# Toeplitz passes of a four-layer network kernel moved: the first beside the second half of the projections, the second beside image 0's front, with weights rearranged and its loads on ScalarE's queue

## The chip, the core and the metric

The kernel runs on one core of one Trainium2 chip. The metric is the device time of one execution in microseconds (us). A NeuronCore has TensorE (PE in the profile, with PEld for its weight loads), VectorE (DVE), ScalarE (ACT), GpSimd (POOL) and SyncE (SP); SP, ACT and POOL also issue DMA transfers, each from its own queue, in program order.

## What is computed

The input is eight images of 56 x 56 pixels with 192 channels, in float32. Four residual layers follow one another, each behind a group norm: a Toeplitz gated layer, window attention, a depthwise 3 x 3 convolution, and a selective scan in four directions. The change concerns the first layer and small tables of the second to fourth. The first layer, cut to what matters:

```
def _gn(v, G=32, eps=1e-5): ...          # group norm without scale and shift
p = silu(x @ p_w.T + p_b)                # x is the normalised image
q = silu(x @ q_w.T + q_b)
v = silu(x @ v_w.T + v_b)                # 576 channels each
qv = q * v
o1 = toeplitz(qv along the rows, a1)     # per channel, a 56 x 56 Toeplitz matrix
o2 = toeplitz(qv along the columns, a2)
x  = x + (p * (o1 + o2)) @ o_w.T + o_b
...
x  = x + window_attention(_gn(x))        # 7 x 7 windows, shifted by 3, bias table, mask
x  = x + depthwise_conv3x3(_gn(x))
x  = x + selective_scan_block(_gn(x))    # projection, conv, 4 scans of 3136 steps, 16 states
```

## The kernel before

All data between the stages lies in HBM. The kernel first makes the Toeplitz generators (`ext`, lines 157 to 203), and then works in two halves of the images: `now` is 0 to 3, `later` 4 to 7.

`products` (line 206) makes q * v. For each image it loads x (L217), takes the group norm (`group_stats`, L130 to L150), normalises into `xn` with a row of ones for the bias (L220, L153), and then, for each of 25 token tiles, multiplies 3 x 384 output columns in two steps of the 192 channels (L234, L235), applies Silu on ACT (L236), multiplies on DVE (L237), and stores four tiles at a time to `qv` (L240). Its `yield 4.3` after each token tile hands a cost in us to whoever drives it.

`toeplitz` (line 246) goes over two axes and six blocks of 96 channels. Two rows (or columns) of an image share the 112 partitions. It loads a block of all four images into `tzx` (8 DMAs, L268), and for every 24 channels a block-diagonal tile of generators into `tm` (2 DMAs, L277). Four channels make a unit: four matmuls of 112 x 112 weights with 112 moving columns (L281), then one copy back into `tzx` (L287, in turn on DVE and ACT when it runs alone, on DVE otherwise), and `yield 1.0`. There are 288 units for four images. Both matmul operands are strided: the weights are `t[:, :, c2 + c]` of a tile [112, 112, 24], the moving columns `x[:, :, c]` of a tile [112, 112, 96]. Results go out by 8 DMAs on POOL's queue (L295) per block.

The driver runs `products(now)` and `toeplitz(now)` to their ends, one after the other. Then come the constants of the rest (L302 to L349), and small tables: the attention bias from 98 DMAs on ACT's queue (L360), four mask additions (L365), convolution taps (L379), and borders of the padded images (L392), all in a buffer `slab` that the front uses next.

`front(b)` is image b's way up to the scan, a generator of small steps: `gate` (first layer's end), `attention`, `conv2`, `inner` (projection and convolution of the scan block) and `steps` (its time steps). For b = 0 a driver at the end of the listing runs it with the products and then the Toeplitz of 4 to 7 (`others`): each front step's engine costs, from a table of prices, times 0.55 is what `others` may spend. After that the scan begins, in an order written out by hand (`manual_schedule`), with the fronts of images 1 to 7 fitted between its instructions by the same prices; the change doesn't touch that part. Outside it, a scheduler orders each engine's instructions, so that program order is only near to the source's order.

Image 0's front is compiled through a helper that records prices, so most of its instructions stand under line 83 in the profile.

Of the kernel before, what the change touches and what calls it, by code (L numbers as in the profile page):

```python
# [15 lines left out]
F32 = mybir.dt.float32  # L16
AF = mybir.ActivationFunctionType
# [71 lines left out]
def model(ctx: ExitStack, tc: tile.TileContext, a: dict, out: bass.AP):  # L89
# [40 lines left out]
    def group_stats(x, sp, ps, mean_out, rstd_out):  # L130

        st = sp.tile([CP, 2, NCH, 6], F32, name="gn_st")
        mv = sp.tile([CP, 2, 2], F32, name="gn_mv")
        for k in range(2):
            for j in range(NCH):
                nc.vector.bn_stats(out=st[:, k, j, :], in_=x[:, k, j * CH : (j + 1) * CH])
            nc.vector.bn_aggr(out=mv[:, k, :], in_=st[:, k].rearrange("p j s -> p (j s)"))
        pm = ps.tile([128, 512], F32, name="ps_gn", tag="ps")
        nc.tensor.matmul(pm[:CP, 0:2], gmat, mv[:, :, 0], start=True, stop=True)
        nc.vector.tensor_copy(mean_out, pm[:CP, 0:2])  # L140

        dm = sp.tile([CP, 2], F32, name="gn_dm")
        nc.vector.tensor_sub(dm, mv[:, :, 0], mean_out)
        nc.vector.tensor_mul(dm, dm, dm)
        nc.vector.tensor_add(dm, dm, mv[:, :, 1])
        pv = ps.tile([128, 512], F32, name="ps_gn", tag="ps")
        nc.tensor.matmul(pv[:CP, 0:2], gmat, dm, start=True, stop=True)
        sd = sp.tile([CP, 2], F32, name="gn_sd")
        nc.scalar.activation(sd, pv[:CP, 0:2], AF.Sqrt, bias=eps5[:CP])
        nc.vector.reciprocal(rstd_out, sd)  # L150
# [54 lines left out]
    def products(images, beside):  # L205
        with (
# [8 lines left out]
            for b in images:  # L215
                x = sp.tile([CP, 2, L], F32, name="x0", bufs=1 if beside else 2)
                nc.sync.dma_start(out=x, in_=blocks(a["x"][b]))  # L217
                group_stats(x, sp, ps, stats0[:, b, :, 0], stats0[:, b, :, 1])
                xn = sp.tile([CP + 1, 2, L], F32, name="xn0")
                nc.gpsimd.memset(xn[CP : CP + 1, 1, :], 1.0)  # L220

                for k in range(2):
                    normalize(xn[:CP, k, ::-1], x[:, k], stats0[:, b, k, 0:1], stats0[:, b, k, 1:2])
                for t0 in range(0, L, 512):
# [3 lines left out]
                    for t in range(n_t):  # L228
                        tok = slice(t0 + t * p_t, t0 + (t + 1) * p_t)
                        sl = sp.tile([128, 2 * D1], F32, name="sl", bufs=3)  # L230
# [15 lines left out]
    def toeplitz(images, beside):  # L246
        G = len(images) * (H // 2)
        with (
            tc.tile_pool(name="tz", bufs=2) as sp,
            tc.tile_pool(name="tz_t", bufs=1) as tp,  # L250
            tc.tile_pool(name="tz_ps", bufs=4 if beside else 8, space=PSUM) as ps,
        ):

            tm = [tp.tile([TT, TT, TC], F32, name=f"tm{i}") for i in range(3)]
            for t in tm:
                nc.gpsimd.memset(t, 0.0)
            n_t = 0
            for ax in range(2):
                along_h = "(h u w) c -> u h w c"
                along_w = "(u h w) c -> u w h c"  # L260
                stored = "(w u h) c -> u w h c"
                size = dict(h=H, u=2) if ax == 0 else dict(w=W, u=2)
                for c0 in range(D1 // CP):
                    x = sp.tile([TT, G, CP], F32, name="tzx", bufs=2 if beside else 3)
                    for n, b in enumerate(images):
                        v = qv_d[b][c0].rearrange(along_w if ax else along_h, **size)
                        for u in range(2):
                            nc.sync.dma_start(out=x[u * W : (u + 1) * W, n * 28 : (n + 1) * 28, :], in_=v[u])  # L268
                    for c1 in range(0, CP, TC):
                        t = tm[n_t % 3]  # L270
                        n_t += 1
                        e = ext[1 - ax][(c0 * CP + c1) // TC]

                        src = bass.AP(e.tensor, e.offset, [[TC, W], [1, W * TC]])
                        for u in range(2):
                            dst = t[u * W : (u + 1) * W, u * W : (u + 1) * W, :].rearrange("p i c -> p (i c)")
                            nc.sync.dma_start(out=dst, in_=src)  # L277
                        for c2 in range(0, TC, 4):
                            po = ps.tile([TT, 4, G], F32, name="ps_tz")
                            for c in range(4):  # L280
                                nc.tensor.matmul(  # L281
                                    po[:, c, :], t[:, :, c2 + c], x[:, :, c1 + c2 + c], start=True, stop=True
                                )
                            cs = slice(c1 + c2, c1 + c2 + 4)
                            copy = nc.vector.tensor_copy if (c2 // 4) % 2 or beside else nc.scalar.copy

                            copy(  # L287
                                x[:, :, cs].rearrange("p (b g) c -> p b g c", g=28)[:, :, ::-1, :],
                                po.rearrange("p c (b g) -> p b g c", g=28),
                            )  # L290
                            yield 1.0
                    for n, b in enumerate(images):
                        v = o_d[ax][b][c0].rearrange(stored if ax else along_h, **size)
                        for u in range(2):
                            nc.gpsimd.dma_start(out=v[1 - u], in_=x[u * W : (u + 1) * W, n * 28 : (n + 1) * 28, :])  # L295
# [3 lines left out]
    for stage in (products, toeplitz):  # L299
        for _ in stage(now, False):  # L300
            pass


    with (
# [45 lines left out]


        bias, bmask, masks = carve(slab, PT_, (NH, WS, 2, WS), (4, 6, PT_), (4, PT_))
        nc.sync.dma_start(out=masks, in_=a["masks"])

        nc.gpsimd.memset(bias, 0.0)
        for i in range(WS):
            for u in range(2):
                for j in range(WS):
                    at = (i * 2 + u) * WS + j
                    nc.scalar.dma_start(  # L360
                        out=bias[at : at + 1, :, :, u, :],
                        in_=a["table"][:, WS - 1 - i : 2 * WS - 1 - i, WS - 1 - j : 2 * WS - 1 - j].unsqueeze(0),
                    )
        for m in range(4):
            nc.vector.tensor_add(  # L365
                bmask[:, m],
                bias.rearrange("p a i u j -> p a (i u j)"),
                masks[:, m : m + 1, :].to_broadcast([PT_, 6, PT_]),
            )
        nc.sync.dma_start(out=bmask_d, in_=bmask)  # L370
        ident3, cw2, cw3, dg2, dg3, edge = carve(
            slab, 128, (32,), (C // 32, 3), (DI // 32, 3), (C // 32, 3, 32), (DI // 32, 3, 32), (2, WP)
        )
        nc.sync.dma_start(out=ident3[:CP], in_=a["ident3"])
        for cw, dg, dg_d in ((cw2, dg2, dg2_d), (cw3, dg3, dg3_d)):
            n = cw.shape[1]
            nc.sync.dma_start(out=cw[:CP], in_=a["cw2" if n == C // 32 else "cw3"])
            for dx in range(3):
                nc.vector.tensor_mul(  # L379
                    dg[:CP, :, dx, :],  # L380
                    ident3[:CP].unsqueeze(1).to_broadcast([CP, n, 32]),
                    cw[:CP, :, dx : dx + 1].to_broadcast([CP, n, 32]),
                )
            nc.sync.dma_start(out=dg_d, in_=dg[:CP])

        nc.gpsimd.memset(edge, 0.0)
        for pads in (pad2_d, pad3_d):
            for pad in pads:
                n = CP if pads is pad2_d else 128
                for c in range(0, pad.shape[0], n):  # L390
                    v = pad[c : c + n].rearrange("p (h w) -> p h w", w=WP)
                    nc.scalar.dma_start(out=v[:, 0 : H + 2 : H + 1, :], in_=edge[:n])  # L392
# [807 lines left out]
        with tc.tile_pool(name="ps0", bufs=4 if later else 8, space=PSUM) as ps:  # L1200
            log = costs.setdefault("front", [])
            first, others, spent = front(0), (us for stage in (products, toeplitz) for us in stage(later, True)), 0.0
            while log_of(first, log) is not None:
                spent += 0.55 * sum(cost for _, cost in log[-1])
                while later and spent > 0.0:
                    us = next(others, None)
                    if us is None:
                        break
                    spent -= us
            for _ in others if later else ():  # L1210
                pass
# [213 lines left out]
```

## Time and profile before

| what | value |
|---|---|
| median of 3 runs | 21627.49 us (21618.97 to 21637.12) |
| the profiled execution | 21638.53 us, its span 21636.7 us |
| mean granted TensorE clock | 0.862 of full |
| PE busy | 17516.4 us (81%) |
| POOL busy | 15086.4 us (70%) |
| DVE busy | 15781.2 us (73%) |
| ACT busy | 12150.2 us (56%) |
| first matmul of the scan stage | about 3450 us after the start |

The profile is of one execution. Busy time is the time in which an engine has at least one instruction of the program at work; a busy engine may still be waiting for data inside an instruction. "Idle before" a group of instructions, and what ended it, tells what an engine waited for. PEclk is the TensorE clock granted, as a share of full. A matmul in float32 stands as two records.

### The profile page before, as it was taken

To read this page: it belongs to the slowest core of one execution; us is meant where nothing else is said; L and a number is where in the kernel's file an instruction comes from. 1 tells how busy PE (TensorE), PEld (TensorE's weight loads), DVE (VectorE), ACT (ScalarE), POOL (GpSimd) and SP (SyncE) were. 2 spreads that over 40 slices of the span, in tenths; PEclk is the share of its full clock that TensorE was granted. 3 is DMA by queue.
4 is the path that set the end of the run, shared out by engine and by line. 5 is a ranking of instruction groups with operands and counts; after the bars stand their busy time and mean duration, and the time that the engine had idled before them with its cause. 6 is when DMAs were issued, how large, how long until landed. Compare 5 with 4: busy or idle time off the path is not lost. (4 is left out here: it accounts for less than half of the span.)

```text
span 21636.7 us, 198667 instructions
## 1 busy us (share of the span) xinstructions
PE 17516.4 (81%) x59404; PEld 9109.9 (42%) x59404; DVE 15781.2 (73%) x12469; ACT 12150.2 (56%) x28249; POOL 15086.4 (70%) x9176
## 2 busy tenths in 40 slices
PE   7878678887887788878887888788878888777777
PEld 4845465433443344334433444344433443333333
DVE  2122116986798779967896789778977887788998
ACT  3126113666666666656665667476656665755555
POOL 0000005886788778867886788678877887799998
PEclk9587658988998899888998899889988998888888
DMA  3931676456544655475446654665466546644443
GB/s 87 244 98 39 193 211 176 131 161 211 173 138 145 217 171 148 134 220 174 138 139 206 192 143 126 206 196 146 133 201 195 145 132 189 202 134 132 138 137 115
DMA packets 2566491, 3470.12 MB, mean 160 GB/s; under 512 B 936270, under 2 KB 2518704, under 8 KB 2534578
## 3 DMA queue, kind: packets, MB, share of 16 engines
q1 hardware_dynamic: 2542724, 3340.61, 52.0%
q0 software_dynamic: 15520, 116.14, 1.5%
q8 instruction: 473, 7.75, 0.2%
q14 instruction: 606, 4.96, 0.1%
q10 hardware_dynamic: 7168, 0.65, 0.0%
HBM read 2822.68 MB, written 634.11 MB: 160 GB/s over the span
## 5 line engine op out<-in xcount | busy, mean ns | idle before, releaser
L1106 PE MATMUL ps_y<-hc,ident_sb 128*128 128x448 f32 x21504 | 10046.0, 605 | 966.8 <-POOL hc L1091 957.4
L1059 POOL TENSOR_TENSOR ring<-du,bm 128x896 f32<-128x896 f32 x5376 | 9459.7, 1774 | 1870.1 <-ACT ring L1066 1736.1
L1076 ACT ACTIVATE ps_a<-delta,A_logs_sb 128x449 f32<-128x449 f32 x10752 | 6859.5, 638 | 314.3 <-DVE ring L1085 57.7
L1106 PEld LDWEIGHTS ps_y<-hc,ident_sb 128*128 128x128 f32 x21504 | 4331.0, 211 | 5336.0 <-issue 3600.1
L1085 DVE TENSOR_TENSOR_SCAN ps_a<-ps_a,ring 128x898 f32<-128x898 f32 x2688 | 5429.7, 2020 | 954.6 <-ACT ring L1066 485.6
L1085 DVE TENSOR_TENSOR_SCAN ring<-ps_a,ring 128x898 f32<-128x898 f32 x2688 | 5422.1, 2017 | 488.2 <-ACT state L1098 180.6
L1091 POOL TENSOR_TENSOR hc<-ring,cm 128x896 f32<-128x896 f32 x2688 | 4767.2, 1774 | 898.9 <-DVE ring L1085 497.3
L1091 DVE TENSOR_TENSOR hc<-ps_a,cm 128x896 f32<-128x896 f32 x2688 | 2934.0, 1092 | 950.7 <-PE ps_y L1106 725.3
L1098 ACT COPY state<-ps_a 128x2 f32<-128x2 f32 x2687 | 426.2, 159 | 2932.4 <-DVE hc L1091 2926.2
L287 DVE COPY tzx<-ps_tz 112x448 f32<-112x448 f32 x432 | 269.8, 624 | 1456.4 <-PE ps_tz L281 1261.2
L281 PE MATMUL ps_tz<-tzx,tm 112*112 112x112 f32 x4608 | 1031.4, 405 | 348.6 <-DMA tm<-ext 280.2
L295 POOL DMA_DIRECT2D o<-tzx x192 | 97.3, 513 | 1593.9 <-DVE tzx L287 1510.2
L281 PEld LDWEIGHTS ps_tz<-tzx,tm 112*112 112x112 f32 x4608 | 1021.8, 319 | 389.5 <-issue 385.5
L1098 ACT COPY state<-ring 128x2 f32<-128x2 f32 x2688 | 504.2, 188 | 663.7 <-DVE ring L1085 644.3
L666 PE MATMUL ps_f<-ident_sb,slab 98*98 98x98 f32 x1344 | 333.4, 328 | 628.5 <-ACT slab L659 626.1
L1042 POOL TENSOR_TENSOR du<-delta,xcd 128x448 f32<-128x448 f32 x672 | 659.4, 981 | 19.5 <-DMA slab<-in_w_p_dram 19.4
L83 PE MATMUL ps_f<-slab 96*32 96x448 f32 (+7 forms) x2432 | 604.2, 569 | 71.2 <-DMA slab<-pad 51.5
L1066 ACT COPY ring<-state 128x6 f32<-128x6 f32 x1536 | 292.8, 191 | 629.0 <-POOL ring L1059 627.7
L666 PEld LDWEIGHTS ps_f<-ident_sb,slab 98*98 98x98 f32 x1344 | 205.2, 159 | 1032.7 <-ACT slab L659 813.1
L234 PE MATMUL ps_qv<-wqv,xn 96*128 96x384 f32 (+1 forms) x1200 | 530.1, 525 | 131.1 <-DVE xn L153 67.5
L503 PE MATMUL ps_f<-ident_sb,slab 112*96 112x112 f32 x4704 | 529.1, 267 | 101.0 <-DVE slab L511 53.5
L503 PEld LDWEIGHTS ps_f<-ident_sb,slab 112*96 112x96 f32 x4704 | 506.6, 169 | 240.3 <-issue 105.5
(221 smaller groups left out, 16312.2 us busy)
## 6 DMA issues: line engine op xcount, KB each, us to landing
bm<-bc SPq DMA_DIRECT2D x1792, 448.0 KB
cm<-bc SPq DMA_DIRECT2D x1792, 448.0 KB
xcd<-xc SPq DMA_DIRECT2D x840, 224.0 KB
dl<-slab SPq DMA_DIRECT2D x224, 672.0 KB
delta<-dl SPq DMA_DIRECT2D x224, 672.0 KB
slab<-pad SPq DMA_DIRECT2D x504, 232.0 KB
tzx<-qv SPq DMA_DIRECT2D x192, 588.0 KB
o<-tzx POOLq DMA_DIRECT2D x192, 588.0 KB, 13.8
```

The source lines that it names most:

```text
L83: return f(*args, **kw)
L234: nc.tensor.matmul(pq[:p_t], xn[:CP, 0, tok], wqv[:CP, 0, col], start=True, stop=False)
L281: nc.tensor.matmul(po[:, c, :], t[:, :, c2 + c], x[:, :, c1 + c2 + c], start=True, stop=True)
L503: nc.tensor.matmul(p[:CP, t * TT : (t + 1) * TT], ot[:, n % 2, i, t, c % 2 * CP : c % 2 * CP + CP], ident[:TT, :TT], start=i == 0, stop=i ...
L666: nc.tensor.transpose(p[:PT_, e * PT_ : (e + 1) * PT_], S[:, 3 * g + e, :], ident[:PT_, :PT_])
L1042: nc.gpsimd.tensor_mul(du[:, 0, :], deltas[i][:, d, 1 : CH + 1], xcs.pop((i, d)))
L1059: nc.gpsimd.tensor_mul(hs[:, :, tokens(i)[0]], dus[i, d].to_broadcast([128, NG, CH]), bms[i, k])
L1076: nc.scalar.activation(dA[:, n, :], deltas[i][:, d, at : at + CH + 1], AF.Exp, scale=negA[:, slot, d, c : c + 1])
L1085: nc.vector.tensor_tensor_scan(h, dA, hs, 0.0, ALU.mult, ALU.add)
L1091: (nc.gpsimd if on_pool(d, k) else nc.vector).tensor_mul(hc, h[:, :, tokens(i)[0]], cms[i, k])
L1098: nc.scalar.copy(states[i][:, d, NG * k : NG * k + NG], h[:, :, tokens(i)[2]])
L1106: nc.tensor.matmul(yps[i, d][:, :CH], ident, hcs[g][:, n, :], start=k + n == 0, stop=k + n == NP + NG - 2)
```

## The change

It has six parts.

1. `toeplitz` fetches each generator tile into one of two row tiles `tr`, and POOL copies it into `tm`, [112, 24, 112], so that a channel's weights are contiguous; the fetch is one chunk ahead. A block of `tzx` is loaded when the block before is half done. It has two `tzx` buffers and four PSUM buffers always, and all copies back are on DVE. The queue of its loads is an argument.
2. `products(later)` runs with `toeplitz(now)` fed in between, at 0.47 of its price; each image is normed and normalised in two halves with single buffers.
3. `toeplitz(later)` runs beside `front(0)`, at 0.29 of the front's price, with its loads on ACT's queue.
4. Bias table, masks, taps and borders are made during `products(now)`, in a pool of their own, with the 98 table loads and the borders on POOL's queue.
5. `group_stats` takes one or two blocks of channels.
6. A driver `beside` does the feeding for both.

```
-    def toeplitz(images, beside):
+    def toeplitz(images, queue):
...
+            rows = [tp.tile([TT, TT, TC], F32, name=f"tr{i}") for i in range(2)]
...
+            def fetch(n):
...
+                for u in range(2):
+                    dst = tr[u * W : (u + 1) * W, u * W : (u + 1) * W, :].rearrange("p i c -> p (i c)")
+                    queue.dma_start(out=dst, in_=src)
+                tms[n] = sp.tile([TT, TC, TT], F32, name="tm")
+                nc.gpsimd.tensor_copy(tms[n].rearrange("p c i -> p i c"), tr)
...
+            load(0)
+            fetch(0)
...
+                for c1 in range(0, CP, TC):
+                    fetch(n_t + 1)
+                    t = tms.pop(n_t)
+                    n_t += 1
+                    if c1 == 2 * TC:
+                        load(m + 1)
...
-                                    po[:, c, :], t[:, :, c2 + c], x[:, :, c1 + c2 + c], start=True, stop=True
+                                po[:, c, :], t[:, c2 + c, :], x[:, :, c1 + c2 + c], start=True, stop=True
...
-                            copy = nc.vector.tensor_copy if (c2 // 4) % 2 or beside else nc.scalar.copy
+                        nc.vector.tensor_copy(
...
-    for stage in (products, toeplitz):
-        for _ in stage(now, False):
+        for n, _ in enumerate(products(now, False)):
+            if n == 8:
...
+                            nc.gpsimd.dma_start(
+                                out=bias[at : at + 1, :, :, u, :],
...
+    def beside(work, other, share):
+        due = 0.0
+        for us in work:
+            due += share * us
+            while due > 0.0:
+                due -= next(other, due)
+        for _ in other:
+            pass
+
+    first = toeplitz(now, nc.sync)
+    next(first)
+    beside(products(later, True), first, 0.47)
...
-                    nc.scalar.dma_start(
-                        out=bias[at : at + 1, :, :, u, :],
...
-            first, others, spent = front(0), (us for stage in (products, toeplitz) for us in stage(later, True)), 0.0
-            while log_of(first, log) is not None:
-                spent += 0.55 * sum(cost for _, cost in log[-1])
...
+            priced = (sum(cost for _, cost in log[-1]) for _ in iter(lambda: log_of(first, log), None))
+            beside(priced, toeplitz(later, nc.scalar), 0.29)
```

In `products`, for the images 4 to 7:

```
+                K = 1 if beside else 2
+                for k0 in range(0, 2, K):
+                    x = sp.tile([CP, K, L], F32, name="x0", bufs=1 if beside else 2)
+                    nc.sync.dma_start(out=x, in_=blocks(a["x"][b])[:, k0 : k0 + K])
+                    group_stats(x, sp, ps, stats0[:, b, k0 : k0 + K, 0], stats0[:, b, k0 : k0 + K, 1])
...
+                    if beside:
+                        yield 12.0
```

## The prediction

> **What bounds the kernel now.** I read the page's slices first. The last 34 of 40 look alike: the scan of the selective-scan layer, with POOL, DVE and PE each at 70 to 90%. The change doesn't touch an instruction of it. The first six slices, some 3450 us, look different: POOL and DVE are nearly idle and the granted clock (PEclk) falls to half. I cut them at the borders of the stages in a table of windows. The columns are the stretch, its length, the busy time of PE, PEld, DVE, ACT and POOL, PEclk, the DMA share and GB/s.
>
> ```profile
> core 0: us, PE busy (x) PEld busy (x) DVE busy (x) ACT busy (x) POOL busy (x), PEclk, DMA share, GB/s
> ...
> 86.00:504.00 418.00, 402.63 (x1212) 229.90 (x1212) 112.67 (x168) 153.26 (x307) 5.41 (x2) 0.97 0.32 81
> 504.00:534.00 30.00, 0.00 (x0) 0.00 (x0) 0.00 (x0) 0.00 (x0) 6.90 (x3) 0.50 0.84 195
> 534.00:1112.00 578.00, 510.76 (x2304) 507.90 (x2304) 89.92 (x144) 76.65 (x144) 44.65 (x88) 0.50 0.87 232
> 1112.00:1246.00 134.00, 0.93 (x4) 0.79 (x4) 13.80 (x30) 4.47 (x5) 10.00 (x11) 0.50 0.30 81
> 1246.00:1570.00 324.00, 321.43 (x1395) 194.08 (x1396) 90.28 (x147) 93.14 (x150) 2.91 (x2) 0.97 0.44 106
> 1570.00:2203.00 633.00, 569.90 (x2178) 320.91 (x2179) 159.03 (x327) 387.80 (x1066) 2.71 (x1) 0.80 0.22 54
> 2203.00:2365.00 162.00, 96.52 (x485) 34.41 (x479) 20.78 (x37) 27.57 (x37) 6.90 (x3) 0.74 0.74 197
> 2365.00:2740.00 375.00, 262.78 (x1123) 190.98 (x1124) 52.11 (x86) 56.83 (x71) 12.14 (x24) 0.63 0.66 201
> 2740.00:3175.00 435.00, 324.45 (x1131) 244.28 (x1129) 68.93 (x111) 91.59 (x113) 20.29 (x40) 0.58 0.71 207
> 3175.00:3390.00 215.00, 170.24 (x768) 169.29 (x768) 59.95 (x96) 0.00 (x0) 15.95 (x32) 0.50 0.76 184
> 3390.00:3450.00 60.00, 4.50 (x25) 4.30 (x26) 8.65 (x8) 8.26 (x16) 17.47 (x15) 0.50 0.92 285
> ```
>
> The stages are: products of images 0-3 (PE-bound, DMA a third busy); their Toeplitz products alone (534 to 1112, DMA at 87%); a hole of 134 us; image 0's gate (to 1570) and attention (to 2203) with products of 4-7 mixed in; its convolution, inner projection and steps (to 3175) with Toeplitz of 4-7; that Toeplitz's rest alone; the scan's start. PE's 510 us of the lone Toeplitz are one matmul after another.
>
> The next view is the source view of four lines (min/median/max in ns): the Toeplitz matmul L281, the projection L234, and L503, which has the same 112 moving columns but reads them and its weights contiguously.
>
> ```profile
> L281 PEld LDWEIGHTS ps_tz<-tzx,tm x4608: 293/320/323, 534.2 to 3384.7; 112*112 112x112 f32 x192
> ...
> L234 PE MATMUL ps_qv<-wqv,xn x1200: 482/486/1009, 86.1 to 2201.2; 96*128 96x384 f32 x165, 96*64 96x384 f32 x7
> ...
> L503 PEld LDWEIGHTS ps_f<-ident_sb,slab x672: 159/163/283, 3473.6 to 3844.3; 112*96 112x96 f32 x168
> ...
> L360 ACTq DMA_DIRECT2D slab<-in_table_dram x98: 714/718/1354, 1141.6 to 1238.9; - x98
> ```
>
> An fp32 matmul is two records: 1152 matmuls per four images stand as 2304. L281's weight load never takes under 293 ns, at either clock. Lone Toeplitz records start 220 ns apart at half clock, and also at full clock (57 records in 13.15 us, 2412 to 2436, PEclk 1.00). L503's start 96 ns apart. So L281 is held by its operands' reads, not by the clock. L360 is the hole: 98 tiny loads issued one by one on ScalarE's queue, 97 us, with the Sqrt of image 4's norm behind them. In attention (activation groups by form):
>
> ```profile
> L236 ACT ACT_TABLE_LOAD x38 | 48.8, 1283 | 0.7
> L83 ACT ACT_TABLE_LOAD x36 | 46.2, 1283 | 3.1 <-DVE mxs L83 2.6
> ```
>
> Silu of the products and Exp of attention swap tables, 95 us of ACT.
>
> **What the Trainium skill says.** "SBUF — State Buffer", Door 1, says SBUF lines are 16 bytes and each access that goes to a new line pays; four fp32 is the free stride. L281's weights step 96 bytes and its moving columns 384. The trace agrees for the weights (293 ns against 163). "TensorE: Matmul & The Clock Gate", Part 1, says the clock is half or full, set by how busy PE was in windows of about 3.4 us; the trace agrees (0.50 in the lone Toeplitz, 1.00 where it alternates with dense matmuls at 2412). "DMA: Bandwidth & Descriptors", Issuing engines are not separate DMA queues, says another queue saves the issue time alone; the transfers share the engines. No run here shows it for these loads. "GPSIMD Engine Reference", section 7, prices a widely strided read at 2.9 cycles an element; no copy of this kind is in the trace.
>
> **The change, part by part.** All times are against the profiled execution: 21638.5 us, span 21636.7. The median of the runs, 21627.5, is 11 below.
>
> *Weights rearranged.* POOL copies each 2688-element chunk so that a channel's weights are contiguous. Bounds: 2.3 us (the memset of that size) to 6.5 us (2688 x 2.9 cycles at 1.2 GHz, an estimate from the GPSIMD page). At 5 us, 48 copies a pass are 240 us on a POOL that is under 10% busy here; each is issued a chunk ahead of use, and a chunk is 48 records, at least 9 us of PE, which hides it. Were the cover gone, the cost would be those 240 us. What PE gains: a contiguous load of 112 would take about 175 ns (163 at 96 columns) and no longer binds. The moving columns stay strided. Two records that stood alone at full clock ended 263 ns after their load; L503's end 180 after. That puts the moving side near 180 to 190 ns a record. I take 187; the ends are 96 (as L503) and 220 (no gain). A unit of four matmuls is 8 x 187 = 1.5 us; 288 units are 432 us instead of 507.
>
> *Products 4-7 beside Toeplitz 0-3* (instead of the lone Toeplitz). The changed program's PE order shows 246 units among the 600 product matmuls and 42 after them. Products: 1200 records x 323 ns (their spacing at full clock) = 388. Units among them: 246 x 1.5 = 368. The 42 alone at today's lone pace, since transfers bind there: 578/288 = 2.0 us, 84. Four image starts with single buffers and twice the small norm steps: 20. Sum 860 in place of 578. Transfers are no bound: 0.87 x 578 + 0.32 x 418 = 637 us of DMA. New waits: SP's Toeplitz loads wait for their buffer's stores with the stores of the products behind them, which have two buffers of four token tiles, 28 us of PE, as slack; POOL's stores wait for DVE with the next copy behind them, a chunk ahead. DVE has 288 copies of 625 ns plus products, about 300. ScalarE's copies all go to DVE. Start: 35 for 30 (one POOL copy).
>
> *The hole.* The 98 table loads go to POOL's queue during products 0-3, 98 x 0.51 us (the POOL issue of L295) = 50 us on an idle engine; 97 if uncovered. The masks, taps and borders move there too, on DVE, SP and POOL, all free. What is late next is the landing of the last Toeplitz stores (20 us today), the constants and gate's first loads: 45 in place of 134.
>
> *Gate and attention beside Toeplitz 4-7.* In the PE order the last unit stands before attention's end, so all 288 lie here. PE's own front work, by spacing of records, is 187 + 234 = 421; with 432 of Toeplitz 853. Idle PE today is 957 - 891 = 66; I keep it. ScalarE loses 147 us of Silu and the 95 of tables and gets the loads: 96 of x at 1.4 us and 96 of weights at 0.39 (SP's medians) = 172 us; 324 with back-pressure, SP's sum today. In front of them wait image 0's Exp and Identity; behind those, PE. They are spread singly, so I charge 40. Sum 960 in place of 957. SP's queue loses them, so front loads no longer stand behind them.
>
> *Convolution, inner, steps alone*: 972 today. Off go 350 us of L281's PE time there and 60 of 2290 to 2365, when PE waits for the first Toeplitz load. 560. Bounds: 912, if Toeplitz only filled idle slots; 450, since an undisturbed step took 9 us (2788 to 2797) and they average 31.
>
> *Ends.* The lone rest, 215, goes. The scan's start falls from 60 to 30, as the buffers it waits for are long free.
>
> Sum: 504 + 35 + 860 + 45 + 960 + 560 + 30 = 2994, against 3450: 456 less. 21638.5 - 456 = 21182; less 11: about **21170**.
>
> **Rivals.**
> *The stride stays the bound* (220 ns): no trace row shows strided columns over contiguous weights; two records are thin evidence. 152 us back: 21320.
> *Toeplitz only filled holes*: PE idles 28% from 2203 to 3175 today, on DMA round trips. Then that part takes 912 and the time is 21520. Against it: step 9 us against 31.
> *Reads stop binding at all*, 110 ns: 4608 x 77 ns, of which DMA lets through about two thirds: 240 less, 20930.
> *Slower: the clock.* A Toeplitz record fills about half of its 187 ns at full clock. If the mix counts as too idle, all of it runs at half clock. For it: 0.58 to 0.63 from 2365 on. Against: 1.00 at 2412, where two units alternate with dense matmuls, and 0.97 in the gate. Price: products 1200 x (640 - 323) = 380 us (640 is their spacing at half clock), front matmuls about 300. At all of it 21850; it decides from two thirds (456/680).
>
> **From cases to numbers.** Main case 60%, own range 20990 to 21300; stride 15%; holes 10%; no read bound 7%; clock 8%. The range leaves out the clock case and the main case's tails, 18% in all: from the no-read-bound case to the holes case, 20920 to 21530. 0.2% (43 us) is about what a measurement of this kernel can tell from no change. Faster 0.91, same 0.02, slower 0.07.
>
> **What would show it.** Spacing of Toeplitz records near 187 ns; PEclk above 0.9 in the first mix; no hole after it; no ACT table loads in attention beyond a few; steps near 13 us each; the same 18190 us from the scan's start. If the first mix takes over 1000 us, or the part after attention over 800, my sum is wrong there.

## The result, and the profile after

The changed kernel takes 21494.8 us in the median (21475.5 to 21516.5), the kernel before 21628.6 beside it: a ratio of 0.9937, 95% interval 0.9924 to 0.995. That is 134 us less, where 458 were forecast. The profiled execution took 21516.5 us, its span 21514.7.

The windows of the changed kernel from the first mix on, cut at its own stage borders (columns as before):

```profile
core 0: us, PE busy (x) PEld busy (x) DVE busy (x) ACT busy (x) POOL busy (x), PEclk, DMA share, GB/s
...
516.00:1388.00 872.00, 785.52 (x3205) 608.06 (x3205) 353.47 (x458) 158.57 (x316) 248.77 (x125) 0.93 0.76 184
1388.00:1493.00 105.00, 63.45 (x330) 62.84 (x329) 27.98 (x42) 0.00 (x0) 34.38 (x16) 0.79 0.58 136
1493.00:1541.00 48.00, 0.84 (x5) 0.48 (x3) 1.74 (x7) 1.65 (x2) 13.30 (x10) 0.54 0.76 205
1541.00:1905.00 364.00, 346.79 (x1779) 265.20 (x1780) 105.14 (x170) 52.06 (x65) 79.09 (x38) 0.95 0.70 166
1905.00:2700.00 795.00, 541.91 (x2875) 436.82 (x2873) 199.49 (x395) 195.32 (x761) 188.37 (x106) 0.75 0.52 134
2700.00:3050.00 350.00, 194.74 (x957) 76.57 (x956) 29.18 (x60) 87.05 (x115) 0.00 (x0) 0.75 0.66 188
3050.00:3272.00 222.00, 127.71 (x252) 50.62 (x252) 0.00 (x0) 97.46 (x122) 9.84 (x7) 0.58 0.58 192
```

Set against the sum of the prediction, in us of the profiled executions:

| stage | forecast | measured | off by |
|---|---|---|---|
| to the end of products 0-3 | 504 | 474 | -30 |
| start of the first mix | 35 | 42 | +7 |
| products 4-7 beside Toeplitz 0-3, with its lone tail | 860 | 872 + 105 = 977 | +117 |
| transition | 45 | 48 | +3 |
| gate and attention beside Toeplitz 4-7 | 960 | 364 + 795 = 1159 | +199 |
| convolution, inner, steps alone, scan start | 560 + 30 | 350 + 222 + 15 = 587 | -3 |
| scan stage | 18190 | 18228 | +38 |

The misses sum to 331, which is the difference of 21516.5 to the forecast 21182 within 4 us. Two of them, both in the mixes, make up the error. Attention is the larger: there PE is busy for 542 of 795 us.

The operations themselves came out as they were costed (source view; min/median/max in ns):

```profile
L312 PEld LDWEIGHTS ps_tz<-tzx,tm x4608: 172/193/312, 515.6 to 2660.4; 112*112 112x112 f32 x192
...
L279 POOL COPY tm<-tr x96: 4693/4790/6546, 510.8 to 2632.4; 112x2688 f32<-112x2688 f32 x96
```

L312 is the Toeplitz matmul (L281 before), L279 POOL's copy of the weights; the records of L312 start 192 ns apart at full and at half clock. The copy takes 4.8 us where 5 were taken, and the 98 table loads (L345), 0.65 us each in the median, leave POOL's queue between 38 and 107 us.

What ScalarE waited for, from the first to the last softmax of the changed kernel (1905 to 2687 us), and PE in the same stretch (columns: us in total, times, longest):

```profile
ACT slab L83 <- PE ps_f L83: 294.7, 104, 15.8
ACT slab L83 <- DVE mxs L83: 152.3, 58, 17.9
ACT slab L83 <- issue: 83.9, 17, 14.9
ACT slab L83 <- DMA slab<-x: 41.2, 7, 18.7
...
PE ps_f L83 <- ACT slab L83: 183.1, 31, 23.4
PE ps_tz L312 <- POOL tm L279: 58.9, 9, 16.5
```

PE's idle time there is 248 us, and two waits are nearly all of it: 183 for ScalarE and 59 for weights that POOL hasn't copied. ScalarE in turn waits 152 us for DVE's part of the softmax, spends 84 us between instructions without waiting for data ("issue") and loses 41 on late loads of image 0's strips. In the trace, 83 of the 84 us lie under its own issues of loads. This is the source view of the input blocks' loads on its queue, from 1905 us on:

```profile
L296 ACTq DMA_DIRECT2D tzx<-qv x64: 312/327/15406, 1905.9 to 2587.2; - x64
```

The 64 issues of input blocks in attention sum to 127 us (one held the queue for 15.4), the 64 of weight rows to 31. One turn of the loop, from the timeline of the changed kernel:

```profile
2029.58 0.31 ACTq L277 DMA_DIRECT2D tr<-ext  x1
...
2030.39 0.31 ACTq L277 DMA_DIRECT2D tr<-ext  x1
...
2037.55 9.37 POOL L279 COPY tm<-tr 112x2688 f32<-112x2688 f32 x2 [20.47 <-DMA tr<-ext]
...
2042.31 18.77 PE L312 MATMUL ps_tz<-tzx,tm 112*112 112x112 f32 x96 [6.53 <-POOL tm L279]
...
2061.66 0.18 DVE L83 RECIPROCAL mxs<-mxs 98x6 f32<-98x6 f32 x1
2061.87 1.71 ACT L83 ACTIVATE slab<-slab,mxs 98x98 f32<-98x98 f32 x6 [17.85 <-DVE mxs L83]
```

A row's load leaves ScalarE only behind attention's copies; POOL waits for it; PE stands 6.5 us before the first unit and then runs 96 records; the softmax's reciprocal stands on DVE behind the units' copies back; and ScalarE, which has the next row's load to issue, waits 17.9 us for the reciprocal. So late weights and the units' copies back reach the softmax through DVE too.

### The profile page after: what moved, and what is told of

The parts are those of the page before. It is cut to its first block, busy times and chain, and to the rows that moved or that the text cites. A ratio compares the mean times of both kernels' runs of the same rounds, so it can differ in the third digit from the quotient of the medians.

```text
span 21514.7 us, 198772 instructions
## 1 busy us (share of the span) xinstructions
PE 17346.1 (81%) x59420; PEld 8955.4 (42%) x59420; DVE 15957.1 (74%) x12633; ACT 12003.9 (56%) x28043; POOL 15598.6 (73%) x9378
## 5 line engine op out<-in xcount | busy, mean ns | idle before, releaser
L279 POOL COPY tm<-tr 112x2688 f32<-112x2688 f32 x96 | 458.6, 4799 | 1116.8 <-DMA tr<-ext 642.8
L312 PE MATMUL ps_tz<-tzx,tm 112*112 112x112 f32 x4608 | 925.8, 370 | 183.6 <-POOL tm L279 178.0
L312 PEld LDWEIGHTS ps_tz<-tzx,tm 112*112 112x112 f32 x4608 | 868.8, 202 | 233.3 <-POOL tm L279 185.5
L316 DVE COPY tzx<-ps_tz 112x448 f32<-112x448 f32 x576 | 356.9, 622 | 741.5 <-PE ps_tz L312 715.4
L241 ACT ACTIVATE sl<-ps_qv 128x384 f32<-128x384 f32 x600 | 293.5, 491 | 753.7 <-PE ps_qv L240 609.2
L242 DVE TENSOR_TENSOR qv<-sl 128x576 f32<-128x576 f32 (+1 forms) x200 | 207.7, 1041 | 573.8 <-ACT sl L241 554.5
```

What stands on the lines that cost most here:

```text
L279: nc.gpsimd.tensor_copy(tms[n].rearrange("p c i -> p i c"), tr)
L312: nc.tensor.matmul(po[:, c, :], t[:, c2 + c, :], x[:, :, c1 + c2 + c], start=True, stop=True)
```

## The experiments

Ratios are to the kernel before, timed beside each, with their 95% intervals; the changed kernel's is 0.9937 (0.9924 to 0.995). Us worked out from a difference of two ratios are uncertain by some 40. Stage times are of one trace each. "Softmax" is the stretch from the first to the last of image 0's 32 softmaxes, with the Toeplitz units that ran in it; 782 us and 203 units in the changed kernel.

### Which part brings what

**e1_sp.** All loads of Toeplitz 4-7 on SyncE's queue.

```
-            beside(priced, toeplitz(later, nc.scalar), 0.29)
+            beside(priced, toeplitz(later, nc.sync), 0.29)
```

> Changed kernel with one word changed: the loads of Toeplitz 4-7 (input blocks and weight rows) are issued on SyncE's queue instead of ScalarE's. Theory Q (in the changed kernel each weight row's load waits in ScalarE's order behind image 0's activations, these wait for PE and DVE, and both stand behind the Toeplitz units that wait for the row): the rows land before they are needed, gate and attention beside Toeplitz 4-7 go from 1160 us to 960-1020, the time from 21495 to about 21320 (21280 to 21370). Theory C (the order in which the scheduler placed the units, in clumps of 25 to 96 matmuls inside attention's chain, costs the time whatever queue loads them): the stage stays within 40 us of 1160, time 21455 to 21535. Theory S (SyncE's strip loads and stores now stand behind row loads that wait for a free row buffer): the stage gets longer, time over 21550.

Measured: 0.9856 (0.9843 to 0.987), 21352 us: one word is worth 0.81%, some 175 us by the ratios; in the two traces the scan starts 145 us earlier (3142 for 3287). Softmax took 447 us with 104 units; the other 96 units went behind attention, and that part grew from 600 to 800. Waits of the same stretch (1894 to 2341):

```profile
ACT slab L83 <- PE ps_f L83: 171.9, 132, 7.3
ACT slab L83 <- DVE mxs L83: 84.1, 61, 3.3
ACT slab L83 <- DMA slab<-x: 0.8, 2, 0.6
PE ps_f L83 <- ACT slab L83: 74.7, 27, 5.2
PE ps_tz L312 <- POOL tm L279: 1.0, 1, 1.0
```

ScalarE's issue time is gone, its waits for DVE are 68 us shorter, and PE idles 76 us in place of 248. But the built order (the one that the scheduler makes) changed with the queue, so queue and placement aren't told apart yet.

**e2_serial.** Toeplitz 4-7 to its end before image 0's parts.

```
-            beside(priced, toeplitz(later, nc.scalar), 0.29)
+            for _ in toeplitz(later, nc.sync):
+                pass
+            for _ in priced:
+                pass
```

> Changed kernel with Toeplitz of images 4-7 run to its end before image 0's parts begin, loads on SyncE's queue, so that the trace has each alone. Tells what mixing is worth. Lone Toeplitz: 2.45 us a unit as in the 42 units after the products (1387 to 1490 us) would be 700 us; 1.54 us a unit (192 ns a record) would be 443. Front alone: PE's own work in gate and attention was counted as 421 us; with attention's round trips I expect 600 to 650. If mixing hides what it can (theories Q and C wrong), the two alone sum to 1350 or more against 1160 and the time is about 21690. If the mix is bad, they sum to 1100-1200 and the time is 21435 to 21540.

Measured: 0.9973 (0.9964 to 0.9982), 21608 us. From the start of the second Toeplitz to the scan it took 1860 us, against 1746 in the changed kernel and 1618 in e1_sp: so the change's mix hides 114 us, and e1_sp's 242. The 21608 us lie between the two cases of the expectation. It is the only trace with attention alone. Its softmax stretch, then those of e1_sp and of the changed kernel:

```profile
2392.00:2792.00 400.00, 252.76 (x1222) 143.96 (x1222) 72.81 (x185) 189.34 (x738) 0.00 (x0) 0.59 0.06 11
```

```profile
1894.00:2341.00 447.00, 370.75 (x2052) 279.23 (x2050) 134.52 (x288) 190.63 (x738) 105.75 (x58) 0.78 0.54 128
```

```profile
1905.00:2687.00 782.00, 533.64 (x2849) 433.08 (x2847) 196.31 (x388) 189.92 (x738) 188.37 (x106) 0.75 0.52 135
```

The fourth column's 190 us is the same work of ScalarE in all three. Attention alone leaves PE idle for 147 of 400 us. At 1.54 us a unit (8 records of 192 ns), e1_sp is 160 us of Toeplitz, 211 of attention's own and 76 idle: it filled half of the idle time. The changed kernel is 313, 221 and 248: it filled none and added 100. Attention's own 253 us alone, at a clock of 0.59, is 211 to 221 in the mixes, at 0.75 to 0.78.

**e3_strided.** The weight rows used as they land, no POOL copy.

```
-            rows = [tp.tile([TT, TT, TC], F32, name=f"tr{i}") for i in range(2)]
+            rows = [tp.tile([TT, TT, TC], F32, name=f"tr{i}") for i in range(3)]
...
-                tms[n] = sp.tile([TT, TC, TT], F32, name="tm")
-                nc.gpsimd.tensor_copy(tms[n].rearrange("p c i -> p i c"), tr)
+                tms[n] = tr
...
-                                po[:, c, :], t[:, c2 + c, :], x[:, :, c1 + c2 + c], start=True, stop=True
+                                po[:, c, :], t[:, :, c2 + c], x[:, :, c1 + c2 + c], start=True, stop=True
```

> Changed kernel without the GpSimd copy: the weight rows are used as they land (96-byte steps, as in the kernel before), with three row buffers. If a record's read sets the pace of the mixes, 4608 records cost 28 ns more each (220 for 192): +130 us, 21625; with the part of it that other waits cover, 21550 to 21625. If the chain load - copy - matmul sets it (the copy is 4.8 us a chunk in that chain and holds the row buffer), leaving it out and the third buffer pay for the stride: 21400 to 21500.

Measured: 0.9972 (0.996 to 0.9983), 21604 us: by the ratios the contiguous weights are worth 0.35%, 76 us, less than the 130 of a read that sets the pace everywhere and inside the range given for it. Its weight loads take 293/319/323 ns again (min/median/max), and its records are 220 ns apart. In the first mix PE is busy for 929 us, 80 more than in the changed kernel, but the mix is only 22 longer: the copies shortened PE's work where PE was not always what the stage waited for. The larger part of the loss lies behind, 1842 us from gate to scan against 1746, where the built order moved too (95 units beside the gate for 84). So 76 us is the price of copy, buffers and order together.

**e4_hole.** The kernel before, with only the setup moved into the products of 0-3 (part 4 of the change).

```
-    for stage in (products, toeplitz):
-        for _ in stage(now, False):
-            pass
+        for n, _ in enumerate(products(now, False)):
+            if n == 8:
...
+                            nc.gpsimd.dma_start(
+                                out=bias[at : at + 1, :, :, u, :],
...
+    for _ in toeplitz(now, False):
+        pass
```

> Kernel before with one part of the change alone: mask table, taps and borders set up during the products of images 0-3, the 98 table loads on GpSimd's queue. By the sum of the prediction the hole of 134 us (1112 to 1246) becomes 45: -89 us, 21540. If the hole was there for another wait (last stores, constants, gate's first loads), it stays near 100 and the time near 21600. If the loads on GpSimd delay the products, over 21630.

Measured: 0.9947 (0.9934 to 0.9959), 21550 us: 115 us less. The hole fell from 134 us to 37 (1103 to 1140), and that is nearly all of the gain. The first matmul of the products also came at 40 us in place of 86, as in the changed kernel, but PE then waits 22 us for their weights, the products end 25 us earlier (473 for 498), and of that 9 are left at the end of the Toeplitz (1103 for 1112). Image 0's first load is why the products begin earlier (timelines of SyncE's queue, of the kernel before and of e4_hole):

```profile
34.93 53.24 SPq L217 DMA_DIRECT2D x<-in_x_dram  x3
```

```profile
8.17 0.92 SPq L217 DMA_DIRECT2D x<-in_x_dram  x2
```

In the kernel before the load stands behind the weights and leaves at 35 us. With the setup's pool opened first it leaves at 8. That the pool moved the tile off memory still in use is likely, and wasn't tried.

### Queue or placement

**f1_x_sp and f2_rows_sp.** One kind of load each on SyncE's queue, the other on ScalarE's.

```
-    def toeplitz(images, queue):
+    def toeplitz(images, queue, rowq=None):
...
-                    queue.dma_start(out=dst, in_=src)
+                    (rowq or queue).dma_start(out=dst, in_=src)
...
-            beside(priced, toeplitz(later, nc.scalar), 0.29)
+            beside(priced, toeplitz(later, nc.sync, nc.scalar), 0.29)
```

The last line is f1's; f2 has the two queues the other way round.

> Changed kernel with Toeplitz 4-7's input blocks loaded on SyncE's queue, its weight rows still on ScalarE's. Which of the two kinds of loads costs the time? In the built order this puts 120 units inside attention, as against 192 of the changed kernel and 87 of the run with both on SyncE; the rest stands beside convolution and later. Theory P (placement: attention alone takes 413 us with PE busy for 261 of them, so it has room for some 100 units; with the blocks on ScalarE's queue the scheduler puts 190 there, and each beyond the room costs 1.9 us): as with both on SyncE, ratio to the kernel before 0.984 to 0.988, about 21320 for a kernel before of 21630. Theory Q (the rows behind ScalarE's activations come late and hold PE): near the changed kernel, ratio 0.992 to 0.995, about 21490.

> The converse: weight rows on SyncE's queue, input blocks still on ScalarE's. In the built order 198 units stand inside attention. Theory P (placement): near the changed kernel, ratio 0.992 to 0.996, about 21500. Theory Q (late rows): as with both on SyncE, ratio 0.984 to 0.988, about 21320. In between: both have a part.

Measured: f1 0.9879 (0.9865 to 0.9892), softmax 502 us with 121 units; f2 0.9935 (0.9922 to 0.9947), 816 us with 203 units. The input blocks on ScalarE's queue are what costs; the rows add 0.2% once the blocks are off it, hardly told apart. As the faster run also has fewer units in attention, this fitted placement too, the theory I then held.

**f3_sp45 and f4_sp54.** Both loads on SyncE's queue, other shares: 0.45 for 0.29, and 0.54 for the first mix's 0.47.

```
-            beside(priced, toeplitz(later, nc.scalar), 0.29)
+            beside(priced, toeplitz(later, nc.sync), 0.45)
```

```
-    beside(products(later, True), first, 0.47)
+    beside(products(later, True), first, 0.54)
```

> All loads of Toeplitz 4-7 on SyncE's queue and its share raised from 0.29 to 0.45: the built order has 135 units beside the gate, 129 in attention, 24 beside the convolution (94, 87, 107 at 0.29). By the stage costs measured so far (0.45 us a unit within attention's room, 1.9 beyond; about 1.5 beside the gate; 2.0 beside convolution and steps): gate +62, attention +50, convolution and later -166, sum about -50: ratio 0.983, 21265 for a kernel before of 21630. If units cost the same wherever they stand: 0.9856 again, 21320.

> All loads of Toeplitz 4-7 on SyncE's queue (share 0.29) and the first mix's share raised from 0.47 to 0.54, so that next to no Toeplitz units are left behind the products (42 units and 103 us in the changed kernel). If the mix has room (PE idles 87 of 872 us there), the 41 us that PE waits in the lone tail for an input block go, and part of the mix's idle time: 40 to 60 us off, ratio 0.983, 21265. If transfers bind the first mix (three quarters busy), the same wait comes inside the mix: 0.9856, 21320.

Measured: f3 0.9872 (0.9857 to 0.9887), a miss: it should have gained 50 us on e1_sp and did not. 158 units fell into softmax and took it to 611 us. f4 0.9841 (0.9827 to 0.9854), the fastest kernel here; but its interval meets e1_sp's, and 40 to 60 us were forecast. Its first mix, tail and all, took 951 us where e1_sp's took 974; PE idles 95 us of it in place of 122.

**p1_pin_act and p2_dense.** Loads on ScalarE's queue as in the change, each unit's first matmul kept behind the PE instruction that was written before it, which stops the scheduler from pulling units ahead.

```
-                            nc.tensor.matmul(
+                            mm = nc.tensor.matmul(
...
+                            if pin and c == 0:
+                                tc.keep_in_program_order(mm)
```

p2 gives attention twice the share:

```
+                    yield us * (0.29 if at < 283.0 else 0.6 if at < 620.0 else 0.29)
```

> Changed kernel, both kinds of loads still on ScalarE's queue, but the first matmul of each Toeplitz unit of images 4-7 is kept behind the PE instruction written before it, so that the scheduler can't pull units ahead. The built order has 82 units beside the gate, 97 in attention and 109 after it. Separates queue from placement. Placement alone is the cause: the same as with both loads on SyncE's queue, first to last softmax 440 to 500 us (782 in the changed kernel), ratio to the kernel before 0.984 to 0.988, about 21320 for a kernel before of 21630. ScalarE's queue costs by itself: first to last softmax over 600, ratio 0.990 or more.

> As the run with pinned units on ScalarE's queue, but with attention's part of the share doubled: 82 units beside the gate, 188 in attention, 18 after it. As many as in the changed kernel (192), but in the order in which they are written, singly between attention's steps, not in runs. If the number of units in attention costs the time (3 us for each beyond 104, as the runs so far lie on one line): first to last softmax 700 to 780, ratio 0.993. If the runs of 48 and more records cost it: attention alone is 400, its idle PE takes 100 units, the other 88 cost 1.5 to 2 us each: 580 to 640 us, ratio about 0.987.

Measured: p1 0.9928 (0.9915 to 0.994), softmax 564 us with 110 units; p2 0.9932 (0.9919 to 0.9946), 746 us with 206. Here the placement theory fell. With half of the units moved out of attention, p1 is no faster than p2 or the changed kernel: what attention gives back, the units cost again behind it (789 us against 599). Nor do runs of 48 and more Toeplitz records decide: two thirds of the records in the changed kernel's softmax stand in such runs, none of p1's do. p2 can't tell number from runs: its units were meant to come singly, but 71% of its records stand in runs of 24 or more, as in the changed kernel (74%).

**g3_pin_sp.** p1 with the loads on SyncE's queue, nothing else.

```
-            beside(priced, toeplitz(later, nc.scalar, True), 0.29)
+            beside(priced, toeplitz(later, nc.sync, True), 0.29)
```

> The run with pinned units, loads on SyncE's queue in place of ScalarE's and nothing else: almost the same order on PE (82, 92, 81, 33 units against 82, 97, 76, 33), so that the difference is the queue alone. The pinned run on ScalarE's queue had a ratio of 0.9928; with the first mix's share changed too, SyncE's had 0.9888, of which 0.0015 is that share. If the queue costs by itself: 0.989 to 0.991. If not: 0.992 to 0.994.

Measured: 0.9887 (0.9873 to 0.9901), apart from p1's interval: at nearly one order, the queue is worth 0.41%, some 89 us (the scan starts 62 us earlier in the trace). Softmax took 507 us with 110 units. The built orders are alike, not the same: 200 of g3's 880 Toeplitz records in softmax stand in four runs of 40 to 64, where p1's longest run is 24. The waits of p1, then of g3_pin_sp:

```profile
ACT slab L83 <- POOL tm L279: 20.3, 7, 4.4
ACT slab L83 <- issue: 17.3, 3, 10.6
ACT slab L83 <- DMA tzx<-qv: 14.5, 3, 12.5
ACT slab L83 <- DMA slab<-x: 10.6, 2, 10.4
...
PE ps_f L83 <- ACT slab L83: 135.5, 41, 11.7
```

```profile
ACT slab L83 <- DMA slab<-x: 9.9, 2, 8.6
...
PE ps_f L83 <- ACT slab L83: 92.4, 40, 9.4
```

The three waits that come with the loads (20 + 17 + 15 us) are gone, and PE waits 43 us less for ScalarE.

The runs fall into two groups by the queue of the input blocks, whatever the order. With contiguous weights, a mix of Toeplitz 4-7 and image 0's parts, and no spare loads (the next two runs), the four with the blocks on ScalarE's queue have ratios of 0.9928 to 0.9937 and scan starts of 3287 to 3337 us; the eight with them on SyncE's, some with other shares too, have 0.9841 to 0.9888 and 3124 to 3225.

Of the 0.81% between e1_sp and the change, about half is thus shown to be the queue's. If the queue costs the same in every order, the other half goes with the order that the scheduler builds around the loads. That isn't shown: in softmax ScalarE idles 109 us under its own issues of loads in the changed kernel, and 41 in p1, so the queue may cost more there. f3_sp45, with no unit behind attention, as in the change, but the loads on SyncE's queue, lies between the two (0.9872).

**g1_dup_act and g2_dup_sp.** e1_sp, with a second load of each block to a spare tensor, on ScalarE's queue, and on SyncE's as control.

```
+                        if dup:
+                            nc.scalar.dma_start(out=spare[m][u, n], in_=v[u])
```

> The kernel with both kinds of loads of Toeplitz 4-7 on SyncE's queue (share 0.29), and beside each of the 96 input-block loads a second load of the same block on ScalarE's queue into a spare DRAM tensor that nobody reads and no buffer guards: ScalarE issues what it issued in the changed kernel for the blocks, but never waits for a buffer. The built order on PE is that of the run without the copies (94, 87, 83, 24 units). If the issue itself on ScalarE costs (126.7 us of it in the attention of the changed kernel for 64 loads, 2 us each, with image 0's Exp and copies behind): some 70 us more for the 36 loads that fall there, ratio 0.988 to 0.991 against 0.9856. If the wait for a buffer is what costs: 0.985 to 0.987.

> Control for the run before it: the same spare loads on SyncE's queue. It has their transfers (7 MB) without ScalarE's issue. If transfers are what costs, both are slower alike; if ScalarE's issue costs, this one stays at 0.985 to 0.987.

Measured: 0.9926 (0.9913 to 0.9939) and 0.9912 (0.9898 to 0.9926). They don't answer the question. Free of buffers, ScalarE's spare loads were pulled ahead into the first mix, which then ended at 1642 us in place of 1488, with Silu behind them; gate, attention and the rest took 372, 447 and 794 us, as in e1_sp. The control lost 43, 29 and 54 us there: 96 needless loads cost some 120 to 150 us in either place. Issue time without a buffer's wait is thus not priced in attention.

### Candidates

**p3_pin_sp54, p4_gate, g4_late.** p3 is g3_pin_sp with 0.54 in the first mix; p4 also raises the gate's share; g4 is f4_sp54 with a block's stores written one chunk later.

```
+                    yield us * (0.66 if at < 283.0 else 0.3 if at < 620.0 else 0.29)
```

```
+                    if c1 == TC and held:
+                        store(*held)
```

> Candidate: units pinned, loads on SyncE's queue, share of the first mix 0.54. The built order (82 units beside the gate, 92 in attention, 114 after it) is close to that of the run with both on SyncE and 0.54, which gave a ratio of 0.9841: 0.983 to 0.985, 21280 for a kernel before of 21630. If ratios under 0.982 come out, single units fit better than the scheduler's.

> Candidate: as the one before, but with the share raised beside the gate, so that 174 units stand there, 113 in attention, 1 after it. By the stage costs (about 1.5 us a unit beside the gate, where PE is busy; 2.0 beside convolution and steps): 92 units and 21 in attention cost 140 + 20, 113 after attention give back 226: 65 us less, ratio 0.981, 21220. If transfers bind the gate's mix (Toeplitz of 4-7 run alone took 2.2 us a unit with transfers 85% busy), a unit costs 2.2 to 2.8 there and the ratio is 0.984 to 0.986.

> Candidate: loads on SyncE's queue, first mix's share 0.54, and a block's stores written one weight chunk later, so that on GpSimd's queue the next weight copy no longer stands behind stores that wait for DVE (217 us of such waits in the first mix). If that wait holds PE there (PE waits 69 us for the copied weights, 41 of them at once): 20 to 60 us off 0.9841, ratio 0.981 to 0.983. If the rows' landing binds, not the copy's turn: 0.983 to 0.985.

Measured: p3 0.9888 (0.9875 to 0.9902), a miss; p4 0.9879 (0.9865 to 0.9892), a miss too: its gate took 567 us with 174 units where p3's took 420 with 82, 1.6 us a unit, and the part after attention fell from 771 to 607. That is 10 us net and not told apart. g4 0.985 (0.9836 to 0.9865): no gain over f4. POOL's waits for DVE ahead of stores were 211 us and PE's for copied weights 69, both as in f4. The edit didn't take away the wait that it was meant for, so whether the stores' turn holds the first mix stays open. Pinning loses in two places: g3's gate took 414 us where e1_sp's took 370, and its softmax, at 110 units for 104, had a PEclk of 0.68 for 0.78, with PE busy for 415 us against 371. The lower clock goes with units that come singly (23% of g3's records in softmax stand in runs of 24 or more, 70% of e1_sp's), but isn't shown to come from that: p2_dense, with 71%, had 0.70.

## Why the prediction missed

The direction was right, but the gain was a third of the forecast. That the time fell inside the range is luck: it lies outside the main case's own 20990 to 21300 and near the 21520 of a rival whose mechanism is out. What failed is the idle time of PE in the two mixes, that of gate and attention first. By the steps of the prediction:

- *Weights rearranged.* Right in rate: 192 ns a record for 187, partly by luck, as it rested on two records. The copy took 4.8 us, inside its bounds; the 6.5 was a price of strided reads, and this copy reads in order and strides its writes. The value was put at 152 us if the stride stayed; e3_strided gives 76, as PE wasn't the only limit of the mixes. The rivals of a bound stride and of reads that stop binding are both out.
- *The hole, the transition, the scan's start, the part after attention.* Right: 48 for 45, 15 for 30, 572 for 560. Steps took 222/14 = 16 us each, not 13. That products 0-3 end 24 us earlier (474 for 498; the forecast's border of 504 lies 6 behind their end) wasn't foreseen.
- *Gate and attention.* This step failed. Its PE terms were right: own work 216 + 221 = 437 us (421 forecast), Toeplitz 288 x 1.54 = 443 (432). What failed is the rest: "Idle PE today is 957 - 891 = 66; I keep it", and "They are spread singly, so I charge 40". Idle came to 17 + 248 = 265 us, and 265 + 437 + 443 is within 14 of the measured 1159. The 66 was read from a mix whose partner, the products, issued no loads on ScalarE; and the charge of 40 was too low: 157 us of issue stood in attention, where ScalarE is a link in each softmax, and loads that waited there held up weights, for which PE waited 59 us. Two passages of the Trainium skill bear on it. "DMA: Bandwidth & Descriptors", Issuing engines are not separate DMA queues, says that another queue saves only issue time, "which is usually small relative to the DMA itself": here a block load's issue took 0.33 us in the median but 2 us in the mean, and in a softmax that wasn't small. "PSUM — Partial Sum Buffer", Engine vs sequencer instructions, says that the queues of ScalarE and VectorE are strict first in, first out: the trace agrees, as the reciprocal above, whose last input was ready at 2044.0 us, ran at 2061.7 behind twelve copies. With the loads on SyncE (e1_sp), idle was 17 + 76 = 93 us, but 96 units then stood behind attention at 2.1 us each (800 - 600 us). The queue isn't all of the miss: f3_sp45, with no unit behind attention, took 1076 us from the gate to its last softmax, where the changed kernel took 1146, and PE idled 169 us of it. So 960 was too low for either queue.
- *First mix.* 117 over, a failed term too. PE's work was 786 + 63 = 849 us for 388 + 432 = 820: 29 of it. Idle was 128 us where the sum had 40. Two waits of 41.6 us each for weights are most of it, one in the mix and one in the lone tail. In the tail the trace shows SyncE's eight input-block issues taking 44.8 us from 1396, the rows' loads behind them:

```profile
1396.22 44.81 SPq L296 DMA_DIRECT2D tzx<-qv  x8
...
1456.63 37.21 PE L312 MATMUL ps_tz<-tzx,tm 112*112 112x112 f32 x192 [41.55 <-POOL tm L279]
```

  "Transfers are no bound" held on average (76% busy) and not at the block's border (93 to 97% from 1420 to 1450). That this is what holds the weights is read from the trace; no run takes it away, and a deeper prefetch wasn't tried.
- *Scan stage.* 38 over, not explained. The traces of all runs, whose scan is the same program, show 18183 to 18228 us, so it may be no effect of the change. In the two profiled executions the scan starts 166 us earlier (3287 for 3452), and 122 of these are left at the end.
- *The clock rival* is out: PEclk was 0.93 in the first mix. *Toeplitz only filled holes* is out as worded (572 us where it had 912); its 28% of idle PE was 30% (288 of 972 us). The warnings that I set (first mix over 1000, part after attention over 800) both stayed silent, as none guarded the stage that failed.

If the parts add up, the moved setup (115 us) and the contiguous weights (76) would be 191 us, more than the 134 measured: the new order with loads on ScalarE took back some 57. The intervals bear this out only just: the change without contiguous weights (e3_strided, 0.996 to 0.9983) stands barely apart from the moved setup alone (e4_hole, 0.9934 to 0.9959). With those loads on SyncE the whole is 0.9856, and with 0.54 in the first mix 0.9841 (345 us beside its kernel before), three quarters of the forecast.

## What to carry to other kernels

A load that is moved to another engine's queue is priced by what stands behind it there: where that engine is a link in a latency chain, as ScalarE in a softmax, an issue or a wait of the load can stop the chain (83 us of ScalarE's idle time here), and the loaded data can come late as well. Idle time read from today's mix belongs to today's partner; take it from the chain alone (here 147 us of 400), and ask which of the new partner's instructions land on the chain's engines. When a queue is changed under a scheduler, the order changes with it, so fix the order once before crediting either, and look in the trace how far it is fixed.

## What the runs showed that I had not expected

Work put beside a latency-bound chain can make the chain's own matmuls shorter: attention's took PE 253 us alone at a clock of 0.59, and, by the sum at 1.54 us a unit, 211 beside 104 units at 0.78. About as many units, pinned and mostly single, went with a clock of 0.68. And with the setup's pool opened first the first load left at 8 us in place of 35, but a start that is 46 us earlier was worth only 9 at the end of the next stage, as other waits took its place.
